# Twelve parts of attention placed among the optional expert steps, and a closing by pairs of token tiles

## The chip, the core and the metric

The kernel runs on one core of a Trainium2 chip. Its time is the device time of one execution in microseconds; before the change it is 1947.31 us, the median of three runs (1946.74 to 1948.36). A core has five engines that work side by side, each through its own queue of instructions in order: TensorE (PE; its weight loads are PEld), VectorE (DVE), ScalarE (ACT), GpSimd (POOL) and SyncE (SP), which here mostly issues transfers. Sixteen DMA engines move the data. Semaphores let an instruction of one queue wait for one of another.

## The reference

Two layers are computed over 2048 tokens of 512 features in float32. Each layer multiplies a mixer by the Silu of a feed-forward part and adds the product to its input:

```python
x = L0_attn_x
xn = _layernorm(x, axis=-1)
s = _L0_attn_ref(xn, ...)              # RWKV recurrence
g = _silu(_L0_ffn_ref(xn, ...))        # two experts, one per token
x = x + s * g
xn = _layernorm(x, axis=-1)
s = _L1_attn_ref(xn, ...)              # attention over pooled and near keys
g = _silu(_L1_ffn_ref(xn, ...))        # 2 shared and 16 routed experts
x = x + s * g
return x
```

The change lies in the second layer. Its feed-forward part adds to each token the output of two shared experts and of the four routed experts with the highest scores:

```python
h = relu(einsum('td,ndf->ntf', flat, shared_w1) + shared_b1[:, None, :])
out = flat + einsum('ntf,nfd->td', h, shared_w2) + shared_b2.sum(0)
vals, idx = top_k(sigmoid(flat @ centroids.T) + bias, 4)
gating = zeros_like(scores).at[arange(T)[:, None], idx].set(vals)
gating = gating / clip(gating.sum(-1, keepdims=True), 1e-08)
# for each of the 16 experts
acc + (relu(flat @ w1 + b1) @ w2 + b2) * g[:, None]
```

Its attention has 16 heads. Keys and values of the first 1792 positions are averaged over blocks of 64, so that tokens before the last 256 attend only to pooled keys, and to more of them the later they stand.

## The kernel before

**Tiles of tokens.** The 2048 tokens are 16 tiles of 128 (`NT`). `xT` holds the normed input with features on partitions; attention writes its result for a tile over that tile's columns of `xT` (`values`, L1597). The last two tiles (14 and 15, `FULL`) have their attention done before the stage of this change. Fourteen are left.

**Routed experts.** Rows are sorted by expert into tiles of 128 in the DRAM tensor `xs`. With four experts per token there are at least 64 such tiles (`FULL_TILES`) and at most 80 (`NRT`); how many hold rows depends on the data and is read into `held`. In the profiled execution 74 tiles are loaded and 73 scattered. A step `j` of the loop at L1731 emits `hidden_rows(j)` and then `down_rows` of the tile before:

- `hidden_rows` (L1657) loads the expert's weights (three transfers of 704, 512 and 192 KB and a row of 2 KB, three buffers) and the rows `x` (L1671), transposes `x` on TensorE (`tp`, L1678), copies it on ScalarE (`xg`, L1680), and multiplies by the first weights (`ph`, L1685), with ReLU on ScalarE (`ht`, L942).
- `down_rows` (L1706) multiplies by the second weights (`py`, L1709), scales by the gate on VectorE (`y`, L1714, four buffers) and has GpSimd scatter `y` into two halves of a DRAM tensor `comb` with accumulation (L1717). A scatter into one half starts when the one before it into the same half has landed.

Steps after 64 stand in a branch (`tc.If`, L1735) that each engine takes or skips for itself. The ones after `held` are skipped.

**Attention in parts.** `attention()` (L1599) is a generator with 42 parts for seven blocks of 256 tokens, six to a block: two parts project queries and rotate them (`pq`, L1352, then VectorE with `cs` and `sn`, which SyncE loads at L1343), two compute scores and softmax for one tile each (`ps`, L1560 and L1566; seven VectorE operations and an Exp at L1329), and two apply the values (transposes `pt`, L1585; copy `sT`, L1590; `pw`, L1593; copy into `xT`, L1597). The last two blocks are interleaved: two queries, scores of tiles 10 and 11, two queries, value of 10, scores of 12 and 13, values of 11, 12 and 13. Before the change all parts are taken within the first 64 steps. PSUM has three buffers (`aps`) for all these products.

**Closing.** After the loop, 32 transfers bring the sums in from `comb` (L1758, two halves for each tile). For each tile ScalarE takes the Silu (L1763), VectorE multiplies by the attention's result in `xT` (L1765) and adds the layer's input `xo` (L1768), and SyncE stores the tile (L1769). `xo` is loaded within the loop (L1746).

**What sets the order.** The program is written in one thread of Python; a scheduler places each instruction on its engine's queue by its dependencies and adds the semaphores, so that instructions that depend on nothing near may stand earlier or later than they are written. Branches cut the queues: an instruction is inside one or outside.

Of the kernel before, what the change touches and what calls it, by code (L numbers as in the profile page):

```python
# [9 lines left out]
F32 = mybir.dt.float32  # L10
I32 = mybir.dt.int32
AF = mybir.ActivationFunctionType
ALU = mybir.AluOpType
# [4 lines left out]
P = 128  # L18
T = 2048
D = 512  # L20
NT = T // P
# [35 lines left out]
FULL = (14, 15)  # L57
# [11 lines left out]
NRT = T * KR // P + NR  # L69
# [8 lines left out]
def tile_kernel(ctx: ExitStack, tc: tile.TileContext, a: dict):  # L78
    nc = tc.nc
# [36 lines left out]
    xr1 = dram.tile([T, D], F32, name="xr1")  # L116
# [58 lines left out]
    for i in range(0, NT, 2):  # L175
        xin = n0.tile([P, 2, D], F32, tag="xin", bufs=NT // 2, name="xin")
        nc.sync.dma_start(
            out=xin, in_=a["x"][i * P : (i + 2) * P, :].rearrange("(n p) d -> p n d", p=P)
# [10 lines left out]
        out=wdc, in0=gate0_w[:, :, 1], in1=gate0_w[:, :, 0], op=ALU.subtract  # L189
    )  # L190
    wdp = n0ps.tile([P, NC, P], F32, tag="tp", name="wdp")
    for c in range(NC):
        dg = n0.tile([P, P], F32, tag="dg", bufs=2, name="dg")
        nc.vector.tensor_scalar(
            out=dg, in0=ident, scalar1=wdc[:, c : c + 1], scalar2=None, op0=ALU.mult
# [16 lines left out]
        out=upper, in_=upper, compare_op=ALU.is_gt, fill=0.0, base=0,  # L212
# [7 lines left out]
        out=eno, in0=col[:, 0:NST], scalar1=float(P), scalar2=None, op0=ALU.mult  # L220
# [4 lines left out]
    for i in range(0, NT, 2):  # L225
# [4 lines left out]
            out=shift, in0=mv[:, :, 0], scalar=-1.0, in1=rstd, op0=ALU.mult, op1=ALU.mult  # L230
        )
        for j in range(2):
# [6 lines left out]
                out=junk, in0=xn, in1=wdiff, scale=1.0, scalar=0.0, op0=ALU.mult, op1=ALU.add,  # L239
                accum_out=dl[:, i + j : i + j + 1],  # L240
            )
    for i in range(NT):
# [11 lines left out]
        out=sel[:, :, 0], in0=dl, scalar1=0.0, scalar2=None, op0=ALU.is_le  # L254
    )
    nc.vector.tensor_scalar(
        out=sel[:, :, 1], in0=dl, scalar1=0.0, scalar2=None, op0=ALU.is_gt
# [3 lines left out]
        out=m, in0=dl, scalar=-1.0, in1=dl, op0=ALU.mult, op1=ALU.min  # L261
# [8 lines left out]
    for o, tri in ((0, upper), (N2, sums)):  # L270
        nc.tensor.matmul(
            out=tab[:, o : o + N2], lhsT=tri, rhs=sel.rearrange("p n e -> p (n e)"),
# [7 lines left out]
        out=run.rearrange("p e n -> p (e n)"), data0=newrow.rearrange("p e n -> p (e n)"),  # L280
# [8 lines left out]
        out=full, in0=own.to_broadcast([P, NT // 2]), in1=eno2[:, :, 1], op=ALU.is_gt  # L289
# [4 lines left out]
        out=paired[:, 0:1], in0=paired[:, 1:2], scalar1=2.0 * P, scalar2=None, op0=ALU.mult  # L294
    )
    nc.vector.tensor_tensor(
        out=pair_e[:, 0 : NSP - 1], in0=eno2[0:1, :, 0],
        in1=paired[0:1, 0:1].to_broadcast([1, NSP - 1]), op=ALU.is_ge,
    )
    nc.vector.tensor_tensor(  # L300
        out=pair_e[:, NSP - 1 : NSP], in0=own[0:1, :], in1=paired[0:1, 0:1], op=ALU.is_le
    )
    nc.vector.tensor_scalar(
        out=paired[:, 1:2], in0=paired[:, 0:1], scalar1=-1.0, scalar2=float(T),
# [4 lines left out]
        out=run[:, 1, :], in0=run[:, 1, :], scalar1=paired[:, 0:1], scalar2=None, op0=ALU.add  # L309
# [3 lines left out]
        out=row, in0=within, in1=run.rearrange("p e n -> p n e"), op=ALU.add  # L313
# [3 lines left out]
        out=alone, in0=row[:, :, 0], scalar1=paired[:, 0:1], scalar2=paired[:, 1:2],  # L317
# [10 lines left out]
        out=past, in0=bc(rowf, 2, C3), in1=bc(eno, 1, C3), op=ALU.is_ge  # L328
# [6 lines left out]
        out=place, in0=at, scalar=float(-P), in1=rowf, op0=ALU.mult, op1=ALU.add  # L335
# [12 lines left out]
    for i0 in range(0, NT, HN):  # L348
# [3 lines left out]
            in1=bc(col, 1, [P, HN, P]), op=ALU.is_equal,  # L352
# [1179 lines left out]
    m1t = ctx.enter_context(tc.tile_pool(name="m1t", bufs=1, space=PSUM))  # L1532
    aq = ctx.enter_context(tc.tile_pool(name="aq", bufs=1))
    aq2 = ctx.enter_context(tc.tile_pool(name="aq2", bufs=2))
    fin = ctx.enter_context(tc.tile_pool(name="fin", bufs=NT))
    tiles = ExitStack()
    m1w = tiles.enter_context(tc.tile_pool(name="m1w", bufs=3))
    m1f = tiles.enter_context(tc.tile_pool(name="m1f", bufs=1))
# [167 lines left out]
    def down_rows(j, w, hT, g, to):  # L1706
# [13 lines left out]
            )  # L1720

    FULL_TILES = T * KR // P
    att = list(range(6 * (FULL[0] * P // QB)))
    attend = attention()
    rest_of = {}
    held = nc.values_load(
        tiles_n[0:1, 0:1], min_val=FULL_TILES, max_val=NRT,
        skip_runtime_bounds_check_because="it is a sum of counts, FULL_TILES to NRT",
    )
    pending, taken = None, 0  # L1730
    for j in range(NRT + 1):  # L1731

        with contextlib.ExitStack() as more:
            if j > FULL_TILES:
                more.enter_context(tc.If(held > j - 1))  # L1735
            made = hidden_rows(j) if j < NRT else None
            if taken < len(att) and (j + 1) * len(att) // FULL_TILES > taken:
                next(attend)
                taken += 1
            if pending is not None:  # L1740
                down_rows(*pending)
            pending = (j, *made) if made is not None else None
            i = j - (FULL_TILES - NT)
            if 0 <= i < NT:
                xo = fin.tile([P, D], F32, tag="xo", name="xo")
                nc.sync.dma_start(out=xo, in_=xr1[i * P : (i + 1) * P, :])  # L1746
                rest_of[i] = xo
    assert next(attend, None) is None

    tiles.close()  # L1750
    fin2 = ctx.enter_context(tc.tile_pool(name="fin2", bufs=NT))


    sums_of = {}
    for i in range(NT):
        y = fin2.tile([P, D], F32, tag="y", name="y")
        for h, c_ in enumerate(comb):
            nc.sync.dma_start(  # L1758
                out=y[:, h * D // 2 : (h + 1) * D // 2], in_=c_[i * P : (i + 1) * P, :]
            )  # L1760
        sums_of[i] = y
    for i, y in sums_of.items():
        nc.scalar.activation(y, y, AF.Silu)  # L1763
        y4 = y.rearrange("p (c t) -> p c t", t=P)
        nc.vector.tensor_tensor(  # L1765
            out=y4, in0=xT[:, :, i * P : (i + 1) * P], in1=y4, op=ALU.mult
        )
        nc.vector.tensor_tensor(out=y, in0=y, in1=rest_of[i], op=ALU.add)  # L1768
        nc.sync.dma_start(out=a["out"][i * P : (i + 1) * P, :], in_=y)  # L1769


# [91 lines left out]
```

## Time and profile before

| quantity | value |
|---|---|
| median of three runs | 1947.31 us |
| the profiled execution: time | 1949.3 us |
| the profiled execution: span | 1947.6 us |
| PE busy | 1846.0 us (95%) |
| DVE, ACT, POOL busy | 784.7, 527.8, 466.1 us |
| `ph` L1685, PE | 1776 matmuls, 213.9 us |
| `py` L1709, PE | 438 matmuls, 207.6 us |
| scatter `comb<-y,to` L1717, POOL | 146 instructions of 1557 ns, 227.4 us |
| GpSimd idle before them, waiting for an earlier scatter | 140.5 us |
| `y` L1714, DVE | 73 of 748 ns |
| first routed `y`, last routed `y` done | 1354.42, 1894.09 us |
| first load of the sums issued | 1917.61 us |
| mean TensorE clock granted | 0.98 |

A row such as `L1714 DVE TENSOR_SCALAR y<-py,g 128x512` names the source line, the engine, the operation and its output and inputs. In the chain of waits a line gives start, length and what the end of the kernel hung on at that time; DMA there means that a transfer was on its way, and a name with q (SPq, POOLq) the queue of that engine itself. A window gives the busy time of each engine between two times, with the granted clock of TensorE (1.00 is full), the share in which the DMA engines were occupied, and what they moved in GB/s. An engine is idle "before" an operation while it waits for the releaser named.

### The profile page before, as it was taken

The numbers are of one execution on the slowest core, as the hardware profiler recorded it, in microseconds if no ns is written. First come the engines' busy times: TensorE is split into PE (matmuls) and PEld (weight loads), VectorE is DVE, ScalarE is ACT, GpSimd is POOL, SyncE is SP. The second block draws the span as 40 slices with busy tenths as digits, with TensorE's granted clock in tenths as the row PEclk, the third lists the DMA queues.
The fourth block names the chain that finished last, engine by engine and source line by source line (L and its number), as shares of the span: only waits on it lengthen the run. The fifth ranks groups of instructions, "written<-read, shape, count | busy, mean of one in ns | idle before, by whom it ended". The sixth has DMA issues, their size and how long they took to land.

```text
span 1947.6 us, 23278 instructions
## 1 busy us (share of the span) xinstructions
PE 1846.0 (95%) x8107; PEld 1287.3 (66%) x8107; DVE 784.7 (40%) x1581; ACT 527.8 (27%) x997; POOL 466.1 (24%) x350
## 2 busy tenths in 40 slices
PE   5899999999999999999989999999999999999990
PEld 4677777777877777777534744445777777777660
DVE  8713536272725444341276444321332333232213
ACT  6213232232423232321234122221222222222222
POOL 1301112120212010110300561000434443333341
PEclk9899999999999999999999999999999999999995
DMA  7557785625563443437451652025999999888896
GB/s 252 204 172 246 243 288 194 215 94 177 164 224 106 152 141 118 131 126 276 130 182 55 219 191 84 31 81 173 289 311 325 270 279 265 247 250 245 223 273 189
DMA packets 214609, 381.36 MB, mean 196 GB/s; under 512 B 17484, under 2 KB 134988, under 8 KB 213592
## 3 DMA queue, kind: packets, MB, share of 16 engines
q1 hardware_dynamic: 184408, 332.78, 51.3%
q0 software_dynamic: 28784, 45.63, 10.6%
q10 hardware_dynamic: 1296, 1.41, 0.2%
q8 instruction: 67, 1.10, 0.2%
q14 instruction: 54, 0.44, 0.1%
HBM read 294.04 MB, written 85.72 MB: 195 GB/s over the span
## 4 chain that ended last, share of the span: by engine, by line
PE 84%; DMA 6%; DVE 3%; issue 2%; POOL 2%; ACT 2%; SPq 1%; DVEq 0%; POOLq 0%; ACTq 0%
PE pg L571 23%; PE py L593 12%; PE ph L1685 9%; PE py L1709 9%; PE proj L416 7%; PE py L1105 4%; PE ph L956 3%; DMA comb<-y,to 3%; PE pq L1352 2%; PE pw L1593 2%; PE tp L1678 1%; PE ps L1560 1%; PE po L712 1%; PE ps L1566 1%; PE pl L870 1%
## 5 line engine op out<-in xcount | busy, mean ns | idle before, releaser
L571 PE MATMUL pg<-xg,w 128*128 128x256 f32 (+1 forms) x2304 | 495.0, 367 | 3.7 <-ACT xg L563 3.7
L571 PEld LDWEIGHTS pg<-xg,w 128*128 128x128 f32 x2304 | 419.0, 190 | 94.6 <-issue 42.1
L1717 POOL DMA_INDIRECT comb<-y,to x146 | 227.4, 1557 | 343.0 <-DMA comb<-y,to 140.5
L593 PE MATMUL py<-wd,hT 128*128 128x512 f32 x544 | 256.9, 593 | 2.8 <-DVE hT L578 2.8
L1685 PEld LDWEIGHTS ph<-xg,w 128*128 128x128 f32 (+1 forms) x1776 | 202.3, 182 | 37.6 <-ACT xg L1680 31.4
L1685 PE MATMUL ph<-xg,w 128*128 128x128 f32 (+1 forms) x1776 | 213.9, 277 | 1.6 <-DMA w<-in_w_dram 1.6
L1709 PE MATMUL py<-w,ht 128*128 128x512 f32 (+1 forms) x438 | 207.6, 593 | 0.0
L578 DVE TENSOR_TENSOR hT<-sg,pg 128x256 f32<-128x256 f32 (+1 forms) x144 | 56.9, 400 | 335.8 <-ACT sg L576 335.7
L576 ACT ACTIVATE sg<-pg 128x256 f32<-128x256 f32 (+1 forms) x144 | 53.5, 372 | 416.8 <-PE pg L571 416.5
L1714 DVE TENSOR_SCALAR y<-py,g 128x512 f32<-128x512 f32 x73 | 54.6, 748 | 247.6 <-PE py L1709 247.4
L593 PEld LDWEIGHTS py<-wd,hT 128*128 128x128 f32 x544 | 102.1, 190 | 72.1 <-issue 62.0
L942 ACT ACTIVATE ht<-ph,b1t 128x128 f32<-128x128 f32 (+1 forms) x222 | 81.3, 366 | 178.6 <-PE ph L1685 154.2
L1709 PEld LDWEIGHTS py<-w,ht 128*128 128x128 f32 (+1 forms) x438 | 76.7, 191 | 56.2 <-issue 54.0
L1680 ACT COPY xg<-tp 128x512 f32<-128x512 f32 x74 | 43.3, 586 | 179.9 <-PE tp L1678 176.5
L1105 PE MATMUL py<-w,hT 128*128 128x512 f32 (+1 forms) x192 | 89.3, 596 | 0.0
L956 PE MATMUL ph<-xT,w 128*128 128x512 f32 (+1 forms) x192 | 88.0, 597 | 0.0
L1043 POOL DMA_INDIRECT xs<-acc,slot x64 | 63.0, 985 | 67.1 <-DMA xs<-acc,slot 42.8
L712 PE MATMUL po<-wo,yb 128*128 128x512 f32 x128 | 58.4, 612 | 7.6 <-ACT acc L721 3.7
L416 PE MATMUL proj<-xm,wr 128*128 128x256 f32 x256 | 60.5, 391 | 4.3 <-ACT v L452 4.3
L464 POOL TENSOR_TENSOR ex<-st_p,qt 128x1024 f32<-128x1024 f32 x8 | 18.3, 2288 | 193.0 <-DVE qt L463 193.0
L1678 PEld LDWEIGHTS tp<-ident,x 128*128 128x128 f32 x296 | 36.7, 140 | 38.8 <-issue 20.8
L545 POOL DMA_INDIRECT xr<-in_x_dram,tok x17 | 23.2, 1367 | 160.3 <-PE tp L560 133.2
(417 smaller groups left out, 2198.3 us busy)
## 6 DMA issues: line engine op xcount, KB each, us to landing
w<-in_w_dram SPq DMA_DIRECT2D x76, 704.0 KB
w<-in_w_dram SPq DMA_DIRECT2D x76, 512.0 KB
w<-in_w_gate_dram SPq DMA_DIRECT2D x72, 512.0 KB
w<-in_w_up_dram SPq DMA_DIRECT2D x72, 512.0 KB
wd<-in_w_down_dram SPq DMA_DIRECT2D x72, 512.0 KB
xs<-zero SPq DMA_DIRECT2D x16, 1360.0 KB
x<-xs SPq DMA_DIRECT2D x74, 272.0 KB
w<-in_w_dram SPq DMA_DIRECT2D x76, 192.0 KB
```

The source lines that it names most:

```text
L416: nc.tensor.matmul(out=ps[:, j, :], lhsT=w_[:, c, (o0 + j) * P : (o0 + j + 1) * P], rhs=xm[:, c, :], start=(c == 0), stop=(c == NC - 1),)
L571: nc.tensor.matmul(out=pg[:, i, 0:n], lhsT=w[:, c, i * FH + f * P : i * FH + (f + 1) * P], rhs=xg[:, c, 0:n], start=(c == 0), stop=(c == N ...
L578: nc.vector.tensor_tensor(out=hT[:, 0:n], in0=sg[:, 0:n], in1=pg[:, 1, 0:n], op=ALU.mult)
L593: nc.tensor.matmul(out=p, lhsT=hT[:, u * P : (u + 1) * P], rhs=wd[:, f, :], start=first_, stop=last_,)
L712: nc.tensor.matmul(out=po, lhsT=yb[:, c, s * P : (s + 1) * P], rhs=wo[:, c, :], start=(c == 0), stop=(c == NC - 1),)
L942: nc.scalar.activation(dst, src, AF.Relu, bias=b)
L956: nc.tensor.matmul(out=ph[0:n, :], lhsT=up(w, f, n, c), rhs=xT[:, c, cols], start=(c == 0), stop=(c == NC - 1),)
L1043: ins = nc.gpsimd.indirect_dma_start(out=xs, out_offset=bass.IndirectOffsetOnAxis(ap=slot[:, i, k : k + 1], axis=0), in_=acc[:, i, :], in_ ...
L1105: nc.tensor.matmul(out=py, lhsT=hT[0:n, e, f, s * P : (s + 1) * P], rhs=down(w, f, n), start=(e == 0 and f == 0), stop=(e == NS - 1 and f ...
L1685: nc.tensor.matmul(out=ph[0:n, :], lhsT=up(w, f, n, c), rhs=xg[:, c, :], start=(c == 0), stop=(c == NC - 1),)
L1709: nc.tensor.matmul(out=py, lhsT=hT[0:n, f, :], rhs=down(w, f, n), start=(f == 0), stop=(f == NF1 - 1),)
L1717: nc.gpsimd.indirect_dma_start(out=c_, out_offset=bass.IndirectOffsetOnAxis(ap=to, axis=0), in_=y[:, h * D // 2 : (h + 1) * D // 2], in_of ...
```

## The change

Thirty of the 42 parts are taken within the first 64 steps, and the last twelve (`LATE`) by the schedule of `parts_by` over the steps from 64 on. In the steps after 64 they are taken outside the branch, after its end. In the built kernel the instructions of these twelve parts are ordered by the scheduler like all others.

The closing works on two tiles at once: eight buffers of 128 x 2 x 512 instead of sixteen of 128 x 512 for `y` and for `xo`, 16 loads of sums instead of 32, and eight Silu, eight multiplications, eight additions and eight stores of twice the size. `xo` is loaded eight times in pairs.

```diff
-    fin = ctx.enter_context(tc.tile_pool(name="fin", bufs=NT))
+    fin = ctx.enter_context(tc.tile_pool(name="fin", bufs=NT // 2))
...
-    att = list(range(6 * (FULL[0] * P // QB)))
+    MAYBE = NRT - FULL_TILES
+    PARTS = 6 * (FULL[0] * P // QB)
+    LATE = 12
...
+    def parts_by(j):
+
+        if j < FULL_TILES:
+            return (j + 1) * (PARTS - LATE) // FULL_TILES
+        return PARTS - LATE + (j - FULL_TILES) * LATE // MAYBE
+
     pending, taken = None, 0
+
+    def attend_by(j):
+        nonlocal taken
+        while taken < parts_by(j):
+            next(attend)
+            taken += 1
+
     for j in range(NRT + 1):
 
         with contextlib.ExitStack() as more:
             if j > FULL_TILES:
                 more.enter_context(tc.If(held > j - 1))
             made = hidden_rows(j) if j < NRT else None
-            if taken < len(att) and (j + 1) * len(att) // FULL_TILES > taken:
-                next(attend)
-                taken += 1
+            if j <= FULL_TILES:
+                attend_by(j)
             if pending is not None:
                 down_rows(*pending)
             pending = (j, *made) if made is not None else None
             i = j - (FULL_TILES - NT)
-            if 0 <= i < NT:
-                xo = fin.tile([P, D], F32, tag="xo", name="xo")
-                nc.sync.dma_start(out=xo, in_=xr1[i * P : (i + 1) * P, :])
+            if 0 <= i < NT and i % 2 == 0:
+                xo = fin.tile([P, 2, D], F32, tag="xo", name="xo")
+                nc.sync.dma_start(
+                    out=xo, in_=xr1[i * P : (i + 2) * P, :].rearrange("(n p) d -> p n d", p=P)
+                )
                 rest_of[i] = xo
+        if j > FULL_TILES:
+            attend_by(j)
     assert next(attend, None) is None
...
-    for i in range(NT):
-        y = fin2.tile([P, D], F32, tag="y", name="y")
+    for i in range(0, NT, 2):
+        y = fin2.tile([P, 2, D], F32, tag="y", name="y")
         for h, c_ in enumerate(comb):
             nc.sync.dma_start(
-                out=y[:, h * D // 2 : (h + 1) * D // 2], in_=c_[i * P : (i + 1) * P, :]
+                out=y[:, :, h * D // 2 : (h + 1) * D // 2],
+                in_=c_[i * P : (i + 2) * P, :].rearrange("(n p) d -> p n d", p=P),
             )
         sums_of[i] = y
     for i, y in sums_of.items():
         nc.scalar.activation(y, y, AF.Silu)
-        y4 = y.rearrange("p (c t) -> p c t", t=P)
+        y4 = y.rearrange("p n (c t) -> p n c t", t=P)
         nc.vector.tensor_tensor(
-            out=y4, in0=xT[:, :, i * P : (i + 1) * P], in1=y4, op=ALU.mult
+            out=y4, in0=xT[:, :, i * P : (i + 2) * P].rearrange("p c (n t) -> p n c t", t=P),
+            in1=y4, op=ALU.mult,
         )
         nc.vector.tensor_tensor(out=y, in0=y, in1=rest_of[i], op=ALU.add)
-        nc.sync.dma_start(out=a["out"][i * P : (i + 1) * P, :], in_=y)
+        nc.sync.dma_start(
+            out=a["out"][i * P : (i + 2) * P, :].rearrange("(n p) d -> p n d", p=P), in_=y
+        )
```

More of the change, by code (lines that the diff above doesn't have):

```diff
@@ L1743, in tile_kernel @@
             i = j - (FULL_TILES - NT)
-            if 0 <= i < NT:
-                xo = fin.tile([P, D], F32, tag="xo", name="xo")
-                nc.sync.dma_start(out=xo, in_=xr1[i * P : (i + 1) * P, :])
+            if 0 <= i < NT and i % 2 == 0:
[3 more added lines that the diff above has]
+                )
                 rest_of[i] = xo
+        if j > FULL_TILES:
+            attend_by(j)
     assert next(attend, None) is None
     tiles.close()
-    fin2 = ctx.enter_context(tc.tile_pool(name="fin2", bufs=NT))
+    fin2 = ctx.enter_context(tc.tile_pool(name="fin2", bufs=NT // 2))
     sums_of = {}
-    for i in range(NT):
-        y = fin2.tile([P, D], F32, tag="y", name="y")
+    for i in range(0, NT, 2):
+        y = fin2.tile([P, 2, D], F32, tag="y", name="y")
         for h, c_ in enumerate(comb):
             nc.sync.dma_start(
-                out=y[:, h * D // 2 : (h + 1) * D // 2], in_=c_[i * P : (i + 1) * P, :]
+                out=y[:, :, h * D // 2 : (h + 1) * D // 2],
+                in_=c_[i * P : (i + 2) * P, :].rearrange("(n p) d -> p n d", p=P),
             )
```

## The prediction

> **What bounds the kernel now.** I read the page's chain by engine first, then the chain of waits of the last 110 us in order of time, then windows of the routed stage, and last the instructions of the closing.
>
> ```profile
> PE 84%; DMA 6%; DVE 3%; issue 2%; POOL 2%; ACT 2%; SPq 1%; DVEq 0%; POOLq 0%; ACTq 0%
> ```
>
> TensorE carries 84% of the chain. The other 16% matters here, because the change lies where the chain leaves TensorE:
>
> ```profile
> 1849.61 1.72 PE py L1709 x4
> ...
> 1854.47 6.34 DMA comb<-y,to
> ...
> 1902.69 14.66 DMA comb<-y,to
> 1917.35 0.02 SPq L1758
> ...
> 1931.32 2.85 DMA y<-comb
> ...
> 1939.05 0.66 DVE y L1768
> ```
>
> In this stretch every piece up to 1852.6 is a matmul. From 1854.47 it is the scatter of expert results (`comb<-y,to`), each of which waits for its predecessor in the same half of `comb`; at 1917.35 SyncE may load the sums, and 30.2 us later the span ends (1947.6).
>
> ```profile
> 1854.00:1866.00 12.00, 12.00 (x73) 8.60 (x73) 2.44 (x10) 3.49 (x9) 6.23 (x4) 1.00 1.07 351
> 1902.00:1914.00 12.00, 0.00 (x0) 0.00 (x0) 0.00 (x0) 0.00 (x0) 6.60 (x5) 0.50 0.49 55
> 1913.00:1914.00 1.00, 0.00 (x0) 0.00 (x0) 0.00 (x0) 0.00 (x0) 0.00 (x0) 0.50 0.00 0
> ```
>
> In these windows (busy PE, PEld, DVE, ACT, POOL, then clock, DMA share, GB/s) TensorE is full in the optional steps and idle from 1896.1 on. After 1913 nothing moves at all: the last scatter has landed, and for about 4.4 us GpSimd still walks through seven skipped steps before the loads are released.
>
> Pairing each eviction `y` (L1714) with its two scatters on GpSimd's timeline: unconditional steps are 5.81 us without a part of attention and mostly 7.3 to 10.5 with one; optional ones are 5.81. A scatter that starts 2.3 us or more after its `y` follows its predecessor by 7.05 us on average (29 cases, 5.1 to 9.3). So the scatter keeps up until step 63, where it starts 3.1 us late, and falls behind in the optional steps: the last `y` is done at 1894.09 and its result is in 23.3 us later.
>
> **The change, part by part.** *Where the parts go.* The source puts twelve parts between the optional steps. In the built kernel's order on each engine they are not there: between the branches stand only expert instructions. Part 31 (8 matmuls of `pq`) and one matmul of part 32 come before the first branch; everything else of parts 32 to 42 comes after the last. So attention is not interleaved with the optional steps but moved behind them.
>
> *What leaves the expert steps.* By the chain's rows: one `pq` 3.46 us, two more 6.92, scores of tiles 10 to 13 3.57 + 3.88 + 4.21 + 4.52, four value parts of 0.44 + 3.44 each, 15.5; together 42.1, less 0.4 for the early matmul: 41.6 us. TensorE was full, so the last `y` moves from 1894.1 to 1852.5. Expert instructions, weight loads and scatters stay as many.
>
> *What the scatter makes of it.* The 63 full steps now average (1803 - 1354)/63, about 7.1 us, against 7.8 before: the scatter's own pace. Its start at step 63 is then 3 to 12 us late; I take 5. Shifting the present release by 41.6 and adding 2 gives 1877.8; I allow one more for denser weight traffic: **release at 1879**, range 1872 to 1895. The seven skips on GpSimd are in it as before.
>
> *Hidden work.* Between 1852.5 and 1879 TensorE does the rest of part 32, scores 10 and 11 and the first new `pq` (3.0 + 3.6 + 3.9 + 3.5 = 14 us). This costs nothing while scatters are outstanding.
>
> *What is queued behind the new waits.* After that everything else stops. VectorE's queue has two closing products, which need loaded `y`, ahead of the softmax of tile 10. ScalarE has six Silu ahead of that tile's Exp. SyncE has `cs` and `sn` of the last queries behind six `y` loads, which wait for all scatters. TensorE's next `pq` needs a PSUM buffer that the softmax frees. So 28 us of matmuls (one `pq` 3.5, two scores 8.7, four values 15.5) run after the release instead of inside the stage.
>
> *The path from the release.* (1) First product: now 5.4 us after the release (1922.76 - 1917.35). A load twice as large and a Silu of twice the elements add about 0.5 each: 6.5. (2) VectorE until tile 10's weights are ready: five closing operations at 1.14 (two of 512 elements start 0.60 apart; softmax rows of 352 and 448 elements differ by 0.10, so 512 elements are 0.53 and 0.07 is fixed), softmax of tile 10 at seven operations 3.2, half of tile 11's 2.1, two rotations 1.3: 12.4. ScalarE's Exp ends two us earlier. (3) TensorE to the last value part at full clock: 0.44 + copy 0.65 + 3.44 + scores 8.7 + three times (0.44 + 0.75 + 3.44) is 27.1, plus 1.4 because the copy of tile 11 stands behind an Exp on ScalarE: 28.5. (4) Copy 0.6 and two products of 1.15: 2.9. (5) Last store: now 5.5 from last VectorE result to end; twice the bytes but no stores queued ahead: 5.0. Sum 55.3 at full clock.
>
> *The clock.* TensorE idles from about 1867 until about 1889.
>
> ```profile
> 52.65 9.95 PE L416 MATMUL proj<-xm,wv 128*128 128x256 f32 x32
> 66.87 6.23 PE L416 MATMUL proj<-xm,wr 128*128 128x256 f32 x16 [4.27 <-ACT v L452]
> 56.00:58.00 2.00, 2.00 (x6) 1.55 (x6) 0.57 (x1) 1.38 (x1) 1.70 (x2) 0.50 1.11 381
> 58.00:60.00 2.00, 2.00 (x10) 1.73 (x9) 0.00 (x0) 0.00 (x0) 1.67 (x3) 0.92 1.03 385
> ```
>
> These are timeline rows after idles early in the kernel and the windows around the first recovery. Work began at 45.8 and the clock is back only in 58 to 60: 12 us busy at 0.50; after the idle of 4.27 it came back about 5 us after 66.87. The Trainium skill, "TensorE: Matmul & The Clock Gate" (Part 1: The HAM clock gate), has about 3.4 us of sustained work for this. By that the slow stretch fits into the `pq` that VectorE's queue covers: nothing. By the rows it is 5 to 12 us, with 2.7 us of gaps: 2.5 to 7 us. I go by the rows: 4.5. Never recovering would add 16 to 22.
>
> *Table sets.* Silu and Exp now alternate: six set loads in the closing instead of one.
>
> ```profile
> 974.77 1.28 ACT L841 ACT_TABLE_LOAD   x1
> 976.07 1.95 ACT L841 ACTIVATE acc<-yg,topw 128x512 f32<-128x512 f32 x3
> 1920.81 1.28 ACT L1763 ACT_TABLE_LOAD   x1 [24.25 <-DMA y<-comb]
> 1922.76 1.29 DVE L1765 TENSOR_TENSOR y<-xT,y 128x512 f32<-128x512 f32 x2 [28.67 <-DMA y<-comb]
> ```
>
> The Trainium skill, "ScalarE: Activation LUTs" (Rules for kernel authors) budgets about 2.7 us per switch and asks to finish one set before the next, which speaks against this order. In the trace the load is 1.28 and the next activation starts 0.02 later: no drain beside it. By the row the five more loads (6.4) lie beside VectorE's queue and matmuls and cost nothing; by the page Exp of tile 10 would be late and I find 3 us more. The row decides; 3 stays in the range.
>
> *Closing by two tiles.* 16 loads instead of 32 at 0.47 from issue to issue: 7.5 us of issue saved, but alone VectorE would still set the end (19.3 us without a gap from 1922.76), saving about 1.1 (16 fixed shares) and losing 1 at the start: between -1 and +2, nothing here, since it lies beside the attention tail. The paired `xo` loads carry the same bytes under full TensorE steps: nothing.
>
> **Sum.** 55.3 + 4.5 = 59.8 us after the release, against 30.2: 29.6 lost; the release 38.3 earlier. Net -8.7 on the profiled 1947.6, span 1938.9. That execution took 1949.3 in all, 2 above the median of 1947.31; I take the difference off the median: **1938.6 us**.
>
> **Rivals.**
> A (0.56), the forecast: 1929 to 1946.
> B (0.17), slower: the scatter becomes the pace of the whole routed stage. For it: it already waits for itself 44 times (140 us), and in steps 10 to 36 it was nearly always busy at 7.39 us a pair. Against it: 7.05 when late. With 69 loaded pairs from 1354.7, three unloaded at 4.5 and 10 us for the last landing and skips, the release is 1854.7 + 69 x (pace - 6.9): 1889 at 7.4, 1900 at 7.55. It sets the release above 7.25, and the kernel is slower above 7.45: at 7.55, 1900 + 59.8, span 1960, time about 1959; at 7.4 it is 1949, no change.
> C (0.10): the gaps keep the clock at half through the tail: 1939 + 16, 1955. For it: the tail's matmuls wait for ScalarE or VectorE at every transpose and every copy; against it: both early recoveries happened across short gaps.
> D (0.17): TensorE warm at once and the scatter no later than before at step 63: release 1876, tail 55: 1931 or somewhat less.
> That the parts interleave as written (TensorE done at 1896, closing beside it, about 1920) I leave at almost nothing, since the built order excludes it.
>
> **Chances.** What can be told from no change here is about 0.2%, 4 us. A below 1943.4 with most of its share, and D: faster 0.62. The edge of A and B near 7.4: same 0.18. B and C: slower 0.20. The range for 8 in 10 takes D's end and C's and half of B's: 1928 to 1955.
>
> **What would show it.** Right: no attention matmul between optional steps; last `y` near 1853; loads of the sums near 1879; TensorE idle some 20 us at clock 0.50, then about 28 us of `pq`, `ps`, `pw` after the release; six table loads. Wrong: `y` steps of 7.4 and more with VectorE waiting for scatters before the optional steps (B); clock 0.50 until the end (C); closing products that do not wait for the loads.

## The result, and the profile after

| | before | after |
|---|---|---|
| median, us (runs) | 1950.55 (8) | 1943.25 (8), 1940.40 to 1956.52 |
| ratio after/before, 95% interval | | 0.9966 [0.9949, 0.9982] |
| profiled execution, us (span) | 1949.30 (1947.6) | 1940.83 (1939.1) |

The changed kernel is about 7 us faster, inside the predicted range and 4.6 us above the predicted 1938.6. A later set of runs (r1, below) gave 1948.91 against 1954.42, ratio 0.9979 [0.9966, 0.9993], so the gain is real and small: 0.2% to 0.3%.

First the page's chain by engine after the change, and the page's row for the scatter on GpSimd, after and then before (busy time, mean ns; then idle time before it, the releaser and its part):

```profile
PE 83%; DMA 6%; DVE 3%; issue 2%; POOL 2%; ACT 2%; SPq 0%; POOLq 0%; ACTq 0%; DVEq 0%
...
L1717 POOL DMA_INDIRECT comb<-y,to x146 | 226.9, 1554 | 300.0 <-DMA comb<-y,to 222.2
```

```profile
L1717 POOL DMA_INDIRECT comb<-y,to x146 | 227.4, 1557 | 343.0 <-DMA comb<-y,to 140.5
```

The shares are almost those of before. What changed is the time in which a scatter waits for an earlier one: 222.2 us, where it was 140.5. TensorE's timeline shows the end of the optional steps and what comes after:

```profile
1859.24 2.92 PE L1685 MATMUL ph<-xg,w 128*128 128x128 f32 x24
1866.81 4.73 PE L1352 MATMUL pq<-xT,wqg 128*128 128x256 f32 x14 [4.65 <-PEq L1749]
...
1878.82 3.62 PE L1352 MATMUL pq<-xT,wqg 128*128 128x256 f32 x16
1892.00 6.23 PE L1352 MATMUL pq<-xT,wqg 128*128 128x256 f32 x16 [9.56 <-DVE wide L1572]
1900.82 1.08 PE L1585 MATMUL pt<-ident,wide 128*128 128x128 f32 x4 [2.59 <-DVE wide L1335]
1902.58 6.05 PE L1593 MATMUL pw<-vo,sT 128*128 128x512 f32 x8 [0.67 <-ACT sT L1590]
```

Attention begins again only behind the last optional step, as the built order had it. The 4.65 us before it are TensorE's own walk through seven skipped branches. Then a `pq` waits 9.56 us for VectorE and takes 6.23 us at a granted clock of 0.50, where the `pq` ahead of it took 3.62. SyncE's and VectorE's timelines show what it waited for:

```profile
1881.53 3.01 SPq L1777 DMA_DIRECT2D y<-comb  x6
1884.58 0.47 SPq L1343 DMA_DIRECT2D cs<-in_cos_dram  x1
```

```profile
1889.15 2.36 DVE L1785 TENSOR_TENSOR y<-xT,y 128x1024 f32<-128x1024 f32 x2 [15.46 <-ACT y L1783]
1891.43 0.52 DVE L1572 TENSOR_TENSOR wide<-ps,m_pool 128x352 f32<-128x352 f32 x1
```

The sums are loaded from 1881.53; the first closing products follow at 1889.15, and only behind them the softmax of tile 10, whose scores TensorE had finished at 1875.1.

Spans of two executions can't be subtracted as they stand. The first `y` of the routed stage is done at 1354.42 before and at 1361.77 after, although nothing ahead of it was changed; over all profiles of this study it lies between 1354.4 and 1364.5. So the table counts from the first `y`. "Pace" is the mean distance of scatter pairs (of single scatters in r3) over the first 63 steps, whatever each of them waited for, "waits" what VectorE waited for scatters in the 64 full steps, "gaps" TensorE's idle time there that ended on `xg`.

| kernel | pace | waits | gaps | last y | loads released | released to end | first y to end |
|---|---|---|---|---|---|---|---|
| before | 7.82 | 0 | 0 | 539.7 | 563.2 | 30.0 | 593.2 |
| after | 7.19 | 101.5 | 0 | 498.4 | 519.8 | 57.6 | 577.3 |
| after, again (r1) | 7.36 | 115.3 | 5.4 | 506.9 | 529.7 | 57.4 | 587.0 |
| e1 closing alone | 7.82 | 0 | 0 | 539.8 | 564.1 | 29.2 | 593.4 |
| e2 parts alone | 7.22 | 30.9 | 0 | 498.4 | 519.2 | 54.1 | 573.3 |
| parts alone, again (r2) | 7.38 | 106.5 | 7.3 | 508.8 | 531.2 | 54.3 | 585.5 |
| e3 attention first | 7.37 | 114.3 | 4.9 | 508.0 | 530.3 | 44.9 | 575.2 |
| e4 interleaved | 7.45 | 166.2 | 4.5 | 523.8 | 546.8 | 29.0 | 575.8 |
| e5 two queues | 7.47 | 157.1 | 9.9 | 514.2 | 536.4 | 52.8 | 589.2 |
| e6 TensorE filled | 7.43 | 135.4 | 5.9 | 510.8 | 532.6 | 61.0 | 593.6 |
| e7 six y | 7.45 | 14.2 | 0 | 499.8 | 531.0 | 58.0 | 589.0 |
| e8 first, five y | 7.50 | 91.8 | 0.7 | 510.6 | 536.2 | 36.0 | 572.2 |
| e9 early pairs | 7.54 | 123.1 | 1.7 | 508.7 | 535.1 | 40.1 | 575.2 |
| r3 one half | 7.14 | 5.2 | 0 | 498.0 | 515.1 | 57.6 | 572.7 |

From the first `y` on, the change takes 41.3 us out of the expert steps; the release comes 43.4 earlier, the stretch behind it is 27.6 longer, net -15.9 in this execution. In the second profile of the same kernel it is -6.2. The medians say -7.3 and -5.5. In all these profiles with the parts moved, each pair of scatters of steps 1 to 63 starts more than 2.3 us behind the end of its `y`, so the scatter is behind from the first steps on; before the change that holds for 25 of the 63.

### The profile page after: what moved, and what is told of

Read it like the earlier page. It is cut to its first block, busy times and chain, and to the rows that moved or that the text cites. A ratio compares the mean times of both kernels' runs of the same rounds, so it can differ in the third digit from the quotient of the medians.

```text
span 1939.1 us, 23212 instructions
## 1 busy us (share of the span) xinstructions
PE 1857.2 (96%) x8107; PEld 1292.1 (67%) x8107; DVE 787.3 (41%) x1565; ACT 532.9 (27%) x994; POOL 465.9 (24%) x350
## 4 chain that ended last, share of the span: by engine, by line
PE 83%; DMA 6%; DVE 3%; issue 2%; POOL 2%; ACT 2%; SPq 0%; POOLq 0%; ACTq 0%; DVEq 0%
PE pg L571 23%; PE py L593 12%; PE ph L1685 9%; PE py L1709 9%; PE proj L416 7%; PE py L1105 4%; PE ph L956 3%; PE pw L1593 2%; DMA comb<-y,to 2%; PE pq L1352 2%; PE tp L1678 1%; PE po L712 1%; PE ps L1560 1%; PE pl L870 1%; PE pw L1477 1%
## 5 line engine op out<-in xcount | busy, mean ns | idle before, releaser
L1717 POOL DMA_INDIRECT comb<-y,to x146 | 226.9, 1554 | 300.0 <-DMA comb<-y,to 222.2
L1680 ACT COPY xg<-tp 128x512 f32<-128x512 f32 x74 | 43.4, 586 | 177.2 <-PE tp L1678 166.4
L1352 PE MATMUL pq<-xT,wqg 128*128 128x256 f32 x224 | 56.6, 401 | 14.2 <-DVE wide L1572 9.6
```

The lines of the kernel that those rows point to most:

```text
L1352: nc.tensor.matmul(out=pq[:, j, :], lhsT=w[:, c, w0 : w0 + P], rhs=xT[:, c, tc0], start=(c == 0), stop=(c == NC - 1),)
L1717: nc.gpsimd.indirect_dma_start(out=c_, out_offset=bass.IndirectOffsetOnAxis(ap=to, axis=0), in_=y[:, h * D // 2 : (h + 1) * D // 2], in_of ...
```

## The experiments

Each ratio is against runs of the kernel before on the same chip. e1 to e3 shared one chip, e4 to e6 a second, e7 to e9 a third, r1 to r3 a fourth.

### Either half of the change: e1, e2, and again r1, r2

e1 keeps attention where it was and closes by two tiles; e2 moves the parts and closes tile by tile, as before:

```diff
-    for i in range(0, NT, 2):
-        y = fin2.tile([P, 2, D], F32, tag="y", name="y")
+    for i in range(NT):
+        y = fin2.tile([P, D], F32, tag="y", name="y")
...
```

> Before with the closing by two tiles alone; all attention stays among the full steps. My theory: VectorE sets the closing there, and its elements are the same, so -1 to +2 us against before (ratio 0.9995 to 1.001), the loads of the sums at the same distance behind the last y (about 23 us), the stretch from the loads' release to the end about 30 us as before. Rival, that the issue of the loads sets the closing: 16 issues of 0.47 us saved, the stretch after the release 23 to 26 us, ratio 0.996 to 0.998, which would be most of what the whole change gained.

> The changed kernel with its attention parts where they stand, but the closing tile by tile. My theory: the gain is the parts' alone, so within 3 us of the changed kernel (ratio to before 0.9955 to 0.999), with the stretch after the release still about 58 us and TensorE idle and cold at its start. Rival, that the pairs carry the gain: no faster than before (ratio 1.000 or more).

> The changed kernel once more, unchanged, beside its own tile-by-tile form on the same chip. My reading of the runs so far is that the scatter's pace differs from execution to execution (7.19 to 7.54 us a pair in nine traces of the denser stage) and that it sets the release: at 7.2 it comes 520 us after the first y of the stage, at 7.45 some 531 to 536. So the ratio to before lies between 0.995 and 0.998, and the profile has pace and release together: release after the first y = 519.5 + 45 x (pace - 7.19) within 4 us. Rival, that the longer stages of the other runs came from their edits: pace 7.19 and 520 us again.

> The changed kernel with the closing tile by tile once more, beside the changed kernel on the same chip. If the pairs cost what the two profiles showed (57.6 against 54.1 us after the release), this one is 2 to 5 us quicker than the changed kernel, ratio to before 0.993 to 0.996. Rival, that the first difference was one of chips and executions: the same within 2 us.

Measured: e1 0.9989 [0.9979, 1.0000], just under the range I gave, with 29.2 us behind the release, so the pairs alone give nearly nothing. e2 0.9942 [0.9925, 0.9960], a little below the range I gave; beside each other on one chip r1 is 0.9979 [0.9966, 0.9993] and r2 0.9939 [0.9916, 0.9962]. The parts carry all of the gain, and the pairs give part of it back. I had put them at nothing. The timelines say where 3.1 us of it lie (r1 against r2, each from its release). VectorE and then TensorE in r2:

```profile
1897.96 0.69 DVE L1782 TENSOR_TENSOR y<-xT,y 128x512 f32<-128x512 f32 x1 [14.62 <-DMA y<-comb]
1898.57 0.42 DVE L1365 TENSOR_TENSOR qg<-t,t 128x256 f32<-128x256 f32 x1
```

```profile
1899.04 1.54 PE L1566 MATMUL ps<-kd_geo,qg 128*128 128x176 f32 x4 [14.06 <-DVE qg L1365]
...
1906.37 7.07 PE L1352 MATMUL pq<-xT,wqg 128*128 128x256 f32 x32
```

The loads were released at 1892.63, so the first single product follows at +5.3; the first pair in r1 follows at +6.6. In r2 TensorE restarts on scores, and its slow stretch falls on these: `pq` and `pw` behind are at full clock. The last value part ends at +48.9 in r2 and at +50.2 in r1, 1.3 apart. The two last VectorE operations are 0.69 each instead of 1.22, with the copy ahead 2.1 against 3.1, and the last store takes 3.3 against 4.0: 1.1 and 0.7 more. The medians are 7.1 apart; the other 4 us are not explained by these two profiles.

r1 also tests the pace: at 7.36 my line gives 527.4 for the release, measured 529.7, and the run has gaps that the first profile of the same kernel has not. So a longer stage needs no edit. Whether the chip or the single execution sets it is not separated: each set of runs has one profile, and r1's may come from another chip than the first one's.

### What stops TensorE in the full steps: r1's trace, e7, r3

In the first profile after the change TensorE had no gap in the full steps. In r1 it had three. The longest, on VectorE, ScalarE and TensorE, with one window around it (busy PE, PEld, DVE, ACT, POOL, then clock, DMA share, GB/s):

```profile
1593.25 0.16 DVE L1703 TENSOR_TENSOR to<-junk,away 128x1 int32<-128x1 f32 x1 [7.60 <-DMA comb<-y,to]
```

```profile
1594.88 0.36 ACT L1329 ACTIVATE near<-near 128x192 f32<-128x192 f32 x1 [7.79 <-DVE near L1328]
```

```profile
1595.77 4.64 PE L1685 MATMUL ph<-xg,w 128*128 128x128 f32 x20 [4.04 <-ACT xg L1680]
```

```profile
1594.00:1596.00 2.00, 0.23 (x1) 0.23 (x2) 1.43 (x6) 0.84 (x2) 1.13 (x1) 0.50 0.98 344
```

Read from the top: VectorE wants to write `to` and waits 7.60 us for a scatter; a softmax stands behind it, so ScalarE's Exp waits 7.79; the copy of `xg`, which the next expert step needs, stands behind that Exp; TensorE runs dry for 4.04 us and then works at half clock until about 1600.6. That is the scatter setting the pace of the stage, through a chain of three queues. e7 gives the scatter more room, r3 leaves out the second half of the sums:

```diff
-        to = m1x.tile([P, 1], I32, tag="to", bufs=6, name="to")
+        to = m1x.tile([P, 1], I32, tag="to", bufs=10, name="to")
-        y = m1x.tile([P, D], F32, tag="y", bufs=4, name="y")
+        y = m1x.tile([P, D], F32, tag="y", bufs=6, name="y")
```

```diff
-        for h, c_ in enumerate(comb):
+        for h, c_ in enumerate(comb[:1]):
             nc.gpsimd.indirect_dma_start(
```

> The changed kernel with six buffers for y instead of four and ten for to instead of six: expert results may wait longer for their scatter before VectorE has to stop. Theory: with the twelve parts gone the full steps run at the scatter's own pace (7.19 to 7.47 us a pair in the traces so far, by execution), and where it is above about 7.25 VectorE stops for the scatter (101 us of such waits in the changed kernel's profile, none in the one before), softmax and then TensorE with it; more buffers take these waits away (under 15 us) and TensorE has no idle in the full steps, but the release still waits for the scatters, so the time gains little: 0 to 6 us against the changed kernel, ratio to before 0.993 to 0.997. Rival, that the buffers set the pace: the release comes 10 us earlier and the ratio is below 0.992.

> The changed kernel without the scatter of the second half of the columns; everything else, the loads of that half too, stays. It leaves out half of what is summed. Theory: the scatter's pace sets the release. With one scatter a step none is late, VectorE does not stop for one (under 5 us in all), the last y is 498 to 499 us after the first, and the loads are released 11 to 14 us behind it, 509 to 513 us after the first y, against 519 to 536. The stretch after the release stays 56 to 60 us, since its queues are as before. Rival, that the skipped branches and the last landing set the release: 519 us or more as now.

e7: waits 14.2 us, no gap, last y at 499.8, and still the release at 531.0, because the scatter at 7.45 us a pair is late by itself. Ratio 0.9975 [0.9961, 0.9988], just above the range I gave, and no gain that can be told from r1's 0.9979: the buffers are not the limit.

r3: VectorE's waits fall to 5.2 and the last y is at 498.0, but that no scatter would be late was wrong. GpSimd's waits for earlier scatters in these steps, in r3 and then in the changed kernel (us in total, times, longest):

```profile
POOL comb L1717 <- DMA comb<-y,to: 204.1, 37, 8.4
```

```profile
POOL comb L1717 <- DMA comb<-y,to: 200.6, 81, 6.0
```

With one scatter a step the pace is 7.14, beside 7.19 with two. Of the 63 scatters of these steps 60 start 0.73 us behind the landing of the one before, so the chain into one half is as full as with both, and what sets its pace is how long one scatter takes to land. From start to landing that is 6.30 us on average in r3 (pace 7.14), 6.35 in e2 (7.22), 6.51 in r1 (7.36) and 6.61 in e7 (7.45). Why it takes longer in one profile than in another is open. The release at 515.1 is 2 us above what I expected, 14.6 earlier than r1's on the same chip and 4.7 earlier than in the first profile; the stretch behind it stays 57.6. As the pace differs between profiles without any edit, r3 (0.9886 [0.9858, 0.9915], two runs, half of the sums left out) does not say what the second scatter costs.

What ties the release to the scatter is e7, where TensorE is free and the release does not move, and the table: at a pace of 7.19 and 7.22 the loads are released at 519 to 520, at 7.36 to 7.54 at 530 to 536 (e4 apart, see below). The last 8 us of each release are something else. GpSimd's costliest operation in the skipped steps of the changed kernel (ns shortest, median, longest; us from first to last start):

```profile
L1749 POOLq INC_SWDGE_SEM  x7: 847/857/890, 1873.7 to 1880.4; - x7
```

The last scatter starts at 1873.24, GpSimd then walks past its seven skipped steps until 1881.3, and the first load starts at 1881.53. In every profile but e4's the loads start 8.1 to 8.4 us behind the start of the last scatter, before the change too (1909.28 and 1917.61). In r1's trace that scatter has landed 3.7 us after its start; what is left of the time is the walk. No run here shortens it.

### What stands behind the release: e3, e5, e4

e3 keeps every operation and turns the order round in three queues. `behind` orders two instructions on one engine and adds no wait:

```diff
+        newest["ACT"] = nc.scalar.activation(s, s, AF.Exp)
+            newest["DVE"] = nc.vector.tensor_tensor(out=s, in0=s, in1=bc(mx, 2, sh_), op=ALU.mult)
-        cs = pool.tile([P, QB], F32, tag="cs", name="cs")
+        cs = pool.tile([P, QB], F32, tag="cs", bufs=2, name="cs")
+        newest["SP"] = nc.sync.dma_start(out=sn, in_=a["sin"][:, tc0])
...
+            behind(nc.sync.dma_start(
...
+        behind(nc.scalar.activation(y, y, AF.Silu), "ACT")
+        behind(nc.vector.tensor_tensor(
```

e5 is e3 without the changes to SyncE's order and to `cs` and `sn`.

> The changed kernel, with the loads of the sums, each Silu and each first product of the closing held behind the attention that shares their queue, and two buffers for cs and sn. The scatter and the expert steps stay. My theory is that the 58 us after the release are attention that stands behind waits for the sums in the queues of SyncE, ScalarE and VectorE, and a TensorE that has gone cold meanwhile: with the order turned round the softmaxes run while scatters land, TensorE stays at full clock from the last optional step on and ends near 1915 to 1920, and the span near 1925 (-14 us against the changed kernel's 1939, ratio to before about 0.989). Rival, that the stretch is set by the outstanding scatters and the loads behind them rather than by queue order: release at 1881 as now, closing then 30 us behind it or attention no earlier, span 1935 to 1940 and the ratio 0.995 to 0.998 as for the changed kernel.

> Attention first on VectorE and ScalarE alone: each Silu and each first product of the closing stands behind the last softmax, but SyncE keeps the order of the changed kernel (cs and sn of the last queries behind six loads of the sums, one buffer each). Theory: the queue of VectorE is the main price; softmax 10 and 11 run before the release, only the rotations of the last queries wait for cs and sn (release + 6 us), and then 21 us of TensorE, one softmax and the closing products follow: the stretch after the release 44 to 50 us, against 57.6 in the changed kernel and 44.9 with all three queues turned. Rival, that SyncE's order alone makes the wait: 55 to 58 us as in the changed kernel.

e3: 0.9881 [0.9865, 0.9898]; the theory asked for about 0.989. VectorE's timeline in its profile:

```profile
1887.20 0.52 DVE L1579 TENSOR_TENSOR wide<-ps,m_pool 128x352 f32<-128x352 f32 x1 [1.48 <-PE ps L1573]
...
1917.13 1.23 DVE L1792 TENSOR_TENSOR y<-xT,y 128x1024 f32<-128x1024 f32 x1 [0.80 <-ACT y L1790]
```

The loads are released at 1894.85. The softmax of tile 10 starts 7.7 us ahead of that, where in the changed kernel it starts 9.9 us behind it; 12.7 us go from the stretch after the release. This profile is of an execution with gaps in the full steps (1941.40; the five runs span 1926.12 to 1941.40), so the release itself is late in it.

e5: 0.9966 [0.9946, 0.9985], 52.8 us behind the release, more than I expected. The chain of waits and TensorE's timeline:

```profile
1897.12 5.47 DMA cs<-in_cos_dram
```

```profile
1904.60 5.41 PE L1600 MATMUL pw<-vo,sT 128*128 128x512 f32 x8 [7.93 <-DVE t L1371]
```

`cs`, issued behind six loads of the sums, lands at 1902.6, 8.5 us after the first load was issued at 1894.07. The rotations of the last queries wait for it. `pw` of tile 10 starts only when the first of them has been read from PSUM (`t` at L1371 is the second reader of its `pq`), and after 7.93 us of waiting TensorE is slow again, 5.41 instead of 3.70. So SyncE's order, with the second buffers for `cs` and `sn`, is worth 52.8 - 44.9 = 7.9 us: turning two queues of three takes off only 4.8 of the 12.7 us.

e4 asks what the source says literally. The first transpose of each optional step is ordered behind the attention written ahead of it:

```diff
-            nc.tensor.transpose(tp[:, c, :], x[:, c * P : (c + 1) * P], ident)
+            t_ = nc.tensor.transpose(tp[:, c, :], x[:, c * P : (c + 1) * P], ident)
+            if c == 0 and j > FULL_TILES:
+                behind(t_, "PE")
```

> The change as its source reads: the first transpose of each optional step is held behind the attention that the source puts ahead of it on TensorE, so that the twelve parts stand between the branches; the closing is left free. My theory: the release stays where the scatter sets it, about 520 us after the first y of the stage, and attention no longer waits for it, so the stretch after the release falls from 58 us to 40 to 45 and the ratio to before is 0.987 to 0.990, like the run with attention first. Rival, that the twelve parts cost their 42 us wherever they stand among the optional steps, because TensorE is full there: last y near where it was before, release 555 to 560 us after the first y, and the ratio 0.995 to 1.000.

```profile
1831.03 2.92 PE L1694 MATMUL ph<-xg,w 128*128 128x128 f32 x24
1833.79 3.19 PE L1359 MATMUL pq<-xT,wqg 128*128 128x256 f32 x14
```

This is TensorE's timeline: a `pq` now stands between two optional steps. The ratio is 0.9925 [0.9898, 0.9952], between the numbers of the two theories. The stretch behind the release falls to 29.0, lower than I expected, but the release moves to 546.8. SyncE's waits before the first load (us in total, times, longest):

```profile
SPq L1786 <- DMA comb<-y,to: 15.7, 1, 15.7
SPq L1786 <- PEq L1758: 11.7, 1, 11.7
```

The last y is 25.4 us later than in the changed kernel, but the scatter keeps up with it (its last pair starts 1.0 us behind its y), and the wait for it ends at 1896.8, 534.8 after the first y, as in other profiles at this pace. Then SyncE waits 11.7 us more for TensorE, whose skipped branches now stand between the attention parts; in no other run does it. Why it waits there I read from the source and no run shows it: the buffers of the sums take the place of the expert tiles (`tiles.close()`), which TensorE frees behind its last branch. A form without this wait was not run, so e4 is no fair price of attention between the steps.

### The clock: e6

```diff
+    FILL = (10, 4)
+    def fill(n):
+        f = m1y.tile([P, D], F32, tag="py", name="fill")
+        for k in range(n):
+            ins = nc.tensor.matmul(
+                out=f, lhsT=ident, rhs=wqg[:, k % NC, :], start=(k == 0), stop=(k == n - 1)
+            )
...
-        if j > FULL_TILES:
+        if j == NRT:
             attend_by(j)
```

The last lines write all late parts behind the last step, where the built order has nearly all of them anyway.

> The changed kernel with idle TensorE filled: 10 matmuls of 128x512 in f32 (20 passes of about 0.46 us) whose result nobody reads between the two pq parts of the last queries, and 4 more before the transposes of tile 10. They keep the clock up without touching what VectorE waits for. Theory: pq after the release takes 3.5 us instead of 6.23 and pw of tile 10 3.7 instead of 6.05, of which pq lies beside VectorE's queue; the stretch after the release is 2 to 4 us shorter than 57.6. Rival, that the slow clock costs nothing there: pq and pw quicker but the stretch 57 to 58.

TensorE's timeline in e6, and a row of ScalarE's:

```profile
1887.55 8.75 PE L1350 MATMUL fill<-wqg,ident 128*128 128x512 f32 x20
1899.49 5.14 PE L1372 MATMUL pq<-xT,wqg 128*128 128x256 f32 x16 [3.19 <-DVE wide L1597]
...
1913.74 6.53 PE L1620 MATMUL pw<-vo,sT 128*128 128x512 f32 x8 [4.17 <-ACT sT L1617]
```

```profile
1912.15 1.06 ACT L1810 ACTIVATE y<-y 128x1024 f32<-128x1024 f32 x1
```

This run decides nothing. The filling ended 3.2 us before `pq` could start, which ran at 5.14 instead of 3.62. On ScalarE the scheduler put this Silu, with its table load, ahead of the copy `sT`, so that `pw` of tile 10 waited 4.17 us and came 23.9 us after the release instead of 21.1, slow again at 6.53. The ratio is 0.9984 [0.9966, 1.0001]. The price of the clock therefore rests on rows of the changed kernel alone and is not shown by an experiment.

### A version that beats both: e8, e9

e8 is e3 with `bufs=5` for `y` and `bufs=10` for `to`. e9 also puts three closing pairs ahead of the softmax of tile 12:

```diff
+    LAST, EARLY = 5, 3
...
+    for i in range(0, 2 * EARLY, 2):
+        close(i)
+    for _ in range(LAST):
+        next(attend)
...
+        if "CLOSED" in newest:
+            behind(ins, "CLOSED")
```

> Attention first in all three queues, with five buffers for y and ten for to. Here TensorE's attention after the last optional step sets the end, not the release, so a stall in the full steps costs in full. Theory: no stall of TensorE in the full steps, last y 498 us after the first instead of 508, and about 5 to 10 us less than the profile of the run with attention first had; ratio to before 0.984 to 0.988. Rival, that the scatter sets the end here as well: 0.988 to 0.990 as before.

> The run before it, with three of the eight closing pairs put on VectorE and ScalarE between the softmaxes of tiles 11 and 12 instead of behind the last one. Theory: with attention first, VectorE is idle there for 7 us and the closing stands 18 us long behind the last softmax; 6.8 us of it go into that gap, and the end is then set by TensorE: 3 to 6 us less, ratio to before 0.981 to 0.986. Rival, that the sums come too late for the gap: the three products wait for the loads, softmax 12 behind them is late, and the run is no faster or 2 to 5 us slower than the one without.

e8: 0.9881 [0.9863, 0.9900], median 1932.05; e9: 0.9873 [0.9855, 0.9891], median 1929.82. All three forms with attention first beat both kernels by about 1%, and cannot be told apart. e8 ends at the edge of the range I gave and fits its rival, e9 ends above its range. In e8 the last `y` is not at 498: the full steps have 0.7 us of gaps, but from `y` to `y` the nine optional ones take 64.8 us instead of 53.4, with 43.0 us of waits for scatters on VectorE (5.7 in the changed kernel), so one more buffer only moves the stall. In e9 the rival was right; VectorE and TensorE:

```profile
1900.54 1.23 DVE L1794 TENSOR_TENSOR y<-xT,y 128x1024 f32<-128x1024 f32 x1 [8.05 <-ACT y L1792]
```

```profile
1911.30 6.25 PE L1602 MATMUL pw<-vo,sT 128*128 128x512 f32 x8 [6.64 <-ACT sT L1599]
```

With the release at 1894.36 the early products wait 8.05 us for their sums, and a copy that TensorE needs stands behind the Exp of the delayed softmax.

## Why the prediction was right, and where its terms were off

The kernel is faster, for the reason given: the parts do not stand between the optional steps, they stand behind them.

| term | predicted | measured |
|---|---|---|
| TensorE time out of the expert steps | 41.6 | 41.3 |
| release, counted from the first y | 524.6 | 519.8 (r1: 529.7) |
| release to first product | 6.5 | 7.6 |
| to the weights of tile 10 | 12.4 | 11.5 |
| to the end of the last value part, with the clock | 33.0 | 31.3 |
| copy and two products | 2.9 | 3.1 |
| last store | 5.0 | 4.0 |
| release to end | 59.8 | 57.6 |

**The built order.** Right: no attention matmul between optional steps.

**The release.** Forecast A took the scatter's own pace as 7.1 and rival B said that it would rule above 7.25. Both happen. The denser stage runs at 7.19 in one execution of the changed kernel and at 7.36 in another, where VectorE's wait reaches TensorE as B had it. One of B's signs, VectorE waiting for scatters before the optional steps, is there in both (101.5 and 115.3 us), though in the first TensorE's steps stay at 7.06. B's formula gives for 7.36 a release of 1854.7 + 69 x 0.46 = 1886.4, 532.0 after the first `y`, measured 529.7. What I had not seen is that the pace differs between profiles of one kernel; that A's and B's times are mixed within one set of runs, which spans 1940.40 to 1956.52, is likely but not shown, since each set has one profile. I predicted -38.3 for the release; it is -43.4 in one profile and -33.5 in the other. My 7.05 for late scatters, the argument against B, does not come out of the trace as I worded it: before the change the 25 late pairs of the full steps follow the pair ahead of them by 8.0 us on average (5.9 to 10.2), and it is the pairs behind them that follow by 6.9.

**The stretch behind the release.** The queues named in the prediction were the cause, as e3 and e5 show. The 4.5 us for the clock was the term most off here. `pq` lost 6.23 - 3.62 = 2.6 us beside VectorE's work, `pw` of tile 10 lost 6.05 - 3.70 = 2.35 on the path and its transposes 0.5: 2.8 in all. The idle time ahead of it was too long in the forecast: TensorE waited 9.56 us and not some 20, because its walk past the skipped steps (4.65) and a first `pq` of 4.73 kept it until 1882.4. The windows of the changed kernel:

```profile
1894.00:1896.00 2.00, 2.00 (x6) 1.56 (x5) 2.00 (x5) 1.53 (x3) 0.00 (x0) 0.50 1.10 350
1896.00:1898.00 2.00, 2.00 (x8) 1.56 (x6) 2.00 (x4) 1.97 (x3) 0.00 (x0) 0.72 1.07 390
```

TensorE started at 1892.00, and a mean clock of 0.72 in the last window puts the return of the full clock near 1897.1: 5 us of work, not the 12 of the kernel's start that I let weigh in. The Trainium skill, "TensorE: Matmul & The Clock Gate" (Part 1: The HAM clock gate), with some 3.4 us, is nearer than my longer row; what it does not give me is the second loss, after a wait of only 2.6 us.

**Table sets.** Right by the row, with the six loads forecast: in the changed kernel's ScalarE timeline the switch back to Exp is 1.28 and the Exp starts 0.02 later.

```profile
1895.94 1.28 ACT L1329 ACT_TABLE_LOAD   x1
1897.24 0.50 ACT L1329 ACTIVATE wide<-wide 128x352 f32<-128x352 f32 x1
```

**Closing by two tiles, "nothing".** Wrong behind moved attention: 3.1 us in the profiles, more by the medians. With all attention among the full steps it is next to nothing (e1). The step had only looked at the closing where it stood alone, not at its being the head of VectorE's queue and the last thing before the end.

**Interleaving as written, "about 1920".** Too low. e4's profile ends 575.8 after its first `y`, which is 1930.2 on the clock of the execution before. I had put TensorE's end at 1896 with the closing beside it. In e4 the last value part ends at 557.9 after the first `y`, 1912.4 on that clock, and the loads, 29.0 us ahead of the end, waited for TensorE. Neither was in my sum.

**The median.** The profile of after is 8.5 below that of before, near the predicted 8.7, but by luck: a net of -15.9 from the first `y` on and +7.35 ahead of it. That the 1938.6 lies 4.6 below the median measured is in part the base: I took 1947.31 from three runs of the kernel before, and all eight give 1950.55. A change of this size is beyond what one execution of each kernel can tell.

Open: why a scatter takes longer to land in one profile than in another, the 4 us between r1's and r2's medians that their profiles don't show, the clock's price as an experiment, and what shorter walks past skipped steps or more, shorter chains of scatters would give.

## What to carry to other kernels

Before moving work behind a data-dependent stage, list for every queue, the DMA queue too, what stands in front of it there: work that needs nothing from the stage must stand ahead of the first instruction that waits for the stage's result, in all of these queues at once (two of three gave 0.9966, three of three 0.9881). When work is taken out of a stage that hides a serial transfer, compare the new step time with the transfer's own pace, and expect stalls in some runs and not in others, through whatever shares a queue with it, when the two lie as close as 7.06 and 7.19 us do here. Where each piece waits for the landing of the one before, half of the bytes need not be quicker (7.14 in r3). Compare profiles from a point that the change doesn't touch.

## What the runs showed of the hardware

- The scatter's pace is not a constant: 7.19 and 7.36 us a pair in two profiles of the same kernel, 7.19 to 7.54 over eleven profiles with the twelve parts taken out of the full steps. With one scatter a step instead of two it was still 7.14 (r3). It goes with the time that one scatter takes to land, 6.30 to 6.61 us in four profiles.
- A branch that is not taken costs the engine that walks past it: TensorE spent 4.65 us on seven, 0.66 each, before `pq` in the changed kernel (up to 5.92 in e8). GpSimd spent 8.0 us on the same seven, 1.14 each, of which 0.86 is one operation, `INC_SWDGE_SEM`, and the loads of the sums started when it was through (1881.3 and 1881.53).
- The granted clock fell again after 2.6 us of idle time (1898.2 to 1900.8) when it had been full for only about 1 us.
